# A fused attention and triangle kernel: a new loop for the closing stage, and a new order of the last instructions before each triangle stage

## Chip, cores, metric

One Trainium2 chip, one core. The metric is device time in microseconds (us) of one execution. Every number is from runs in the fast state; the mean granted clock of a run was 0.99 to 1.00 in all profiles, though it is lower in some short stretches (one matters below). Engines: PE (matrix), DVE (vector), ACT (scalar), POOL (GpSimd), SP (issues DMAs).

## The reference

Float32 throughout, x is (4, 64, 64, 256): four batches of 4096 tokens. Layer 0 is self-attention over 4096 tokens; layer 1 is a triangle attention over a 64 x 64 grid with eight heads, followed by two layer norms around a small MLP.

```python
# layer 0, per batch
f, g, v = xt @ Wf + bf, xt @ Wg + bg, xt @ Wh + bh
o = softmax(g @ f.T) @ v @ Wo + bo
x = x + o
# layer 1, per batch
q, k, v1, v2 = (x @ W for W in (Wq, Wk, Wv1, Wv2))      # heads of 32
att = softmax(einsum('bilhd,bljhd->biljh', q, k) / sqrt(32), axis=2)
out = einsum('biljh,bilhd,bljhd->bijhd', att, v1, v2)
h = layer_norm(x + out @ Wo)
return layer_norm(relu(h @ W1 + b1) @ W2 + b2 + h)
```

## The kernel before

It goes through the batches one by one: layer 0 (PE bound), then a triangle stage of 32 steps (products on DVE and POOL, PE accumulates). What follows the triangle (output projection, norm, MLP, norm) is done in 16 pieces of 256 tokens, one batch late, in the gaps of the next batch's triangle. Only the last batch has nothing after it to hide in, so its pieces 48 to 63 run in a closing stage, `alone`.

The end of layer 0, where the projections of the last 512 tokens are staged in tiles of tag "R" (three buffers):

```python
stage = [work.tile([P, 4, QB], F32, tag="R", name="stage", bufs=3) for _ in range(3)]
... # cut
score(3)
proj(last, "q", 1, None, stage[1][:, 3, :], nc.scalar)
proj(last, "k", 1, None, stage[2][:, 0, :], nc.scalar)   # stored from the ACT queue
L.fetch_qk(1)
hidden(1)                      # 8 matmuls, 2 relus of an old piece
L.sums(0); L.weights(0)        # softmax sums (DVE), eight scalings (ACT)
proj(last, "v2", 1, None, stage[2][:, 1, :], nc.scalar)
L.turn(0); L.stationary(0)     # transposes (PE), copies attP and wsel (ACT)
```

A product of a triangle step writes a tile of the same tag:

```python
R = work.tile([P, D, N], F32, tag="R", name="R", bufs=3)
nc.vector.tensor_tensor(R, src.unsqueeze(1).to_broadcast([P, D, N]), v2[:, h], ALU.mult)
```

The closing stage, and the tiles that matter in it:

```python
# h: one buffer (tag "h"); z: two (tag "s4"); far loads of A and y: tag "R"
def residue(tt):   # POOL, two instructions
    z = h * lag + (lab + b2)
def finish(tt):    # POOL, two instructions, then a store from SP
    z = z * log + lob
def alone(t0, t1):
    for n in range(2): heads(t0 + 1, n)
    for tt in range(t0 + 2, t0 + 5): load(tt, True)
    stats_a(t0 + 1); roots(0, 2); polish(0, 2, V)
    for tt in range(t0, t1):
        if before: hidden(tt, ...); rectify(tt, ...)            # PE, 4 relus on ACT
        if one:    affine_a(tt + 1)                             # h, ACT
        if before: affine_o(tt - 1); finish(tt - 1)             # z, ACT
        if two:    heads(tt + 2, ...); load(tt + 5, True)       # PE
        if one:    turn(tt + 1); residue(tt + 1)
        outputs(tt, 0); outputs(tt, 1)                          # PE
        if two:    stats_a(tt + 2)
        stats_o(tt)
        roots(k0, 4); polish(k0, 4, V)      # both norms in one go
    ... # cut: the last piece, in two halves
```

In the names of the profile: `heads` is the output projection of a piece (tile hp), `turn` a transpose (htp), `hidden` and `outputs` the two products of the MLP (mp, zp), `rectify` its relus (hid), and `roots` with `polish` makes the factor of a norm (rn).

## Time and profile before

| what | value |
|---|---|
| time, three runs before the prediction | 3957.36, 3961.72, 3963.80 us |
| span of the profiled run | 3958.3 us |
| PE's last accumulation of the triangle to the first outputs of the closing stage | 3768.9 to 3783.6 us |
| first outputs to the end | 3783.6 to 3958.3 us, 174.7 us |

The views that carry the argument (the chain of waits, the timeline, the windows) are in the prediction. A line of the chain has a start, a duration and what held the end at that time. A line of the timeline has a start, a duration, engine, source line and tiles; in brackets how long the engine had idled and who released it. In a window's line, after the span, each engine's busy time is followed by its count.

### The profile page before, as it was taken

Reading aid. Unit: us, or ns where it says so; the run is one execution under the profiler, and the core shown is the slowest. Engines: PE = TensorE matmul, PEld = TensorE weight load, DVE = VectorE, ACT = ScalarE, POOL = GpSimd, SP = SyncE. Lnnn points to the kernel's source line nnn. Section 1 sums busy time; section 2 is a strip of 40 time slices with the busy share of each in tenths; the row PEclk is TensorE's granted clock in tenths of the full one; section 3 lists DMA queues with packets and bytes.
Section 4 is the critical chain, followed back from the end, with each engine's and each line's share of the span. In section 5 each row is a group of like instructions: output and inputs, shape, how many; then the busy total and the mean of one; then the engine's idle time right before and its main releaser. Section 6 shows DMA issues by size and latency. Waiting matters only on the chain.

```text
span 3958.3 us, 59208 instructions
## 1 busy us (share of the span) xinstructions
PE 3742.3 (95%) x23302; PEld 1746.5 (44%) x23302; DVE 2692.7 (68%) x2193; ACT 1812.4 (46%) x3747; POOL 1927.2 (49%) x1024
## 2 busy tenths in 40 slices
PE   9999998889999999998999999999899999999987
PEld 5444444433444444443344444444344444444376
DVE  4444399896445399998444459999644448999944
ACT  3333455554333455554433345555433335555444
POOL 4000098893000199998000049999400008999944
PEclk9999999999999999999999999999999999999999
DMA  4111445552111523323111154233211143331121
GB/s 118 49 51 51 120 131 137 134 146 95 46 53 48 129 66 90 84 52 104 34 51 51 51 135 93 52 84 76 69 51 51 48 110 84 87 85 47 39 74 49
DMA packets 439711, 309.36 MB, mean 78 GB/s; under 512 B 299328, under 2 KB 404544, under 8 KB 432128
## 3 DMA queue, kind: packets, MB, share of 16 engines
q1 hardware_dynamic: 419952, 291.12, 27.8%
q10 hardware_dynamic: 16240, 8.59, 0.8%
q0 software_dynamic: 3232, 5.78, 0.6%
q8 instruction: 186, 3.05, 0.3%
q14 instruction: 101, 0.83, 0.1%
HBM read 165.88 MB, written 139.46 MB: 77 GB/s over the span
## 4 chain that ended last, share of the span: by engine, by line
PE 73%; ACT 8%; DVE 7%; DMA 4%; POOL 3%; issue 3%; SPq 2%; ACTq 0%; POOLq 0%; DVEq 0%
PE o L432 23%; PE acc L808 12%; PE proj L489 8%; PE s L410 7%; PE mp L954 5%; PE zp L969 4%; DVE R L799 4%; PE v1p L514 3%; PE sp L704 3%; POOL Rp L799 3%; ACT S L714 2%; PE hp L861 2%; ACT ao L816 2%; SPq L823 1%; PE y L474 1%
## 5 line engine op out<-in xcount | busy, mean ns | idle before, releaser
L799 POOL TENSOR_TENSOR Rp<-attP,v 128x2048 f32<-128x2048 f32 x328 | 1490.3, 4572 | 459.3 <-ACT attP L758 375.7
L799 DVE TENSOR_TENSOR R<-att,v 128x2048 f32<-128x2048 f32 x696 | 1547.3, 2273 | 102.2 <-ACT attP L758 45.3
L439 DVE TENSOR_TENSOR esum<-esum,e 128x2048 f32<-128x2048 f32 x224 | 512.8, 2289 | 583.4 <-ACT e L421 580.4
L808 PE MATMUL acc<-R,wsel 128*32 128x512 f32 x5568 | 728.3, 605 | 70.5 <-DVE R L799 46.9
L421 ACT ACTIVATE e<-s 128x1024 f32<-128x1024 f32 x512 | 496.6, 1021 | 403.5 <-PE s L410 381.7
L900 POOL TENSOR_SCALAR nt<-mv 128x4 f32<-128x4 f32 (+1 forms) x51 | 9.8, 193 | 1283.6 <-DVE mv L878 1279.5
L816 ACT COPY ao<-acc 128x1024 f32<-128x1024 f32 x256 | 261.4, 1021 | 548.5 <-PE acc L808 462.4
L432 PE MATMUL o<-e,vlo 128*128 128x512 f32 x1024 | 473.7, 605 | 0.0
L432 PE MATMUL o<-e,vhi 128*128 128x512 f32 x1024 | 472.6, 605 | 0.0
L808 PE MATMUL acc<-Rp,wsel 128*32 128x512 f32 x2624 | 346.8, 603 | 34.6 <-POOL Rp L799 34.4
L808 PEld LDWEIGHTS acc<-R,wsel 128*32 128x32 f32 x5568 | 142.6, 109 | 400.2 <-issue 205.0
L432 PEld LDWEIGHTS o<-e,vlo 128*128 128x128 f32 x1024 | 184.0, 189 | 280.8 <-issue 280.8
L432 PEld LDWEIGHTS o<-e,vhi 128*128 128x128 f32 x1024 | 184.3, 189 | 279.7 <-issue 279.7
L410 PE MATMUL s<-gT,fT 32*128 32x512 f32 x2048 | 302.2, 640 | 4.9 <-ACT e L421 4.5
L954 PE MATMUL mp<-hT,w 128*128 128x256 f32 x1024 | 250.5, 390 | 39.3 <-ACT hT L934 39.3
L741 ACT ACTIVATE es<-S,rd 128x64 f32<-128x64 f32 x1024 | 258.4, 338 | 29.3 <-DVE rd L733 28.6
L451 DVE RECIPROCAL rec<-den 128x512 f32<-128x512 f32 x32 | 107.4, 3358 | 215.6 <-PE den L449 215.6
L969 PE MATMUL zp<-w,hid 128*128 128x256 f32 x1024 | 246.2, 386 | 0.6 <-ACT hid L961 0.6
L954 PEld LDWEIGHTS mp<-hT,w 128*128 128x128 f32 x1024 | 182.9, 189 | 117.1 <-ACT hT L934 57.5
L969 PEld LDWEIGHTS zp<-w,hid 128*128 128x128 f32 x1024 | 187.1, 191 | 62.3 <-issue 40.2
L501 ACT COPY st<-proj 128x512 f32<-128x512 f32 x104 | 61.0, 586 | 293.1 <-issue 165.9
L410 PEld LDWEIGHTS s<-gT,fT 32*128 32x128 f32 x2048 | 83.0, 182 | 193.7 <-issue 173.3
(153 smaller groups left out, 3783.9 us busy)
## 6 DMA issues: line engine op xcount, KB each, us to landing
v<-v2d SPq DMA_DIRECT2D x24, 1024.0 KB, 12.3
v1c<-v1d SPq DMA_DIRECT2D x128, 128.0 KB, 2.9
aT<-ao SPq DMA_DIRECT2D x1024, 16.0 KB, 1.9
A<-aT SPq DMA_DIRECT2D x256, 64.0 KB, 2.0
out_dram<-z SPq DMA_DIRECT2D x63, 256.0 KB, 2.2
y<-yT SPq DMA_DIRECT2D x56, 256.0 KB, 2.1
q<-st SPq DMA_DIRECT2D x56, 256.0 KB, 2.6
v1d<-st SPq DMA_DIRECT2D x56, 256.0 KB, 2.1
```

The source lines that it names most:

```text
L410: nc.tensor.matmul(s_ps[r // 2][:, r % 2, :], fT[rows, tt, ts(n, P)], gT[rows, ts(qb, QB)], start=True, stop=not safe,)
L421: nc.scalar.activation(e[g][:, 2 * j : 2 * j + 2, :], s_ps[j], AF.Exp)
L432: nc.tensor.matmul(o_ps[qb], F.v[tt][:, r * 4 + n, :], es[:, r, :], start=(k == 0 and r == 0), stop=(k == 7 and r == 3),)
L439: nc.vector.tensor_tensor(esum[qb], esum[qb], es, ALU.add)
L489: nc.tensor.matmul(ps, w[:, cc, rows], y(qb, cc), start=(cc == 0), stop=(cc == 1))
L514: nc.tensor.matmul(ps[:, ts(n, C)], y(qb, cc)[:, ts(m * 2 + n, P)], wv1_sb[:, cc, :], start=(cc == 0), stop=(cc == 1),)
L741: nc.scalar.mul(self.e[:, i, :], rows[:, i, :], rec[:, i : i + 1])
L799: eng.tensor_tensor(R, src.unsqueeze(1).to_broadcast([P, D, N]), v2[:, h], ALU.mult)
L808: nc.tensor.matmul(acc[32 * c : 32 * c + 32, n % 2, :], w[:, n, c, 16 * h : 16 * h + 32], R[:, ts(c, 8), :].rearrange("p d j -> p (d j)"), ...
L816: nc.scalar.copy(self.ao[step][:, ts(np, 2)].rearrange("p k d j -> p k (d j)"), acc)
L954: nc.tensor.matmul(self.mp[:, fc % 2, :], w1_sb[:, cc, ts(fc, P)], self.hT[tt][:, cc, :], start=(cc == 0), stop=(cc == 1),)
L969: nc.tensor.matmul(self.zp[tt][:, n, :], self.hid[tt][:, fc, ts(n, P)], w2_sb[:, fc, :], start=(fc == 0), stop=(fc == 3),)
```

## The change

Intent: in the closing stage, make the first norm of a piece a whole piece ahead, apart from the second norm of an older piece; load ahead into big tiles that the last heads no longer use; begin on the last piece's first half as soon as it is there. And at the opening of a triangle stage, make the first weights before other work.

```diff
         proj(last, "q", 1, None, stage[1][:, 3, :], nc.scalar)
+        L.sums(0)
         proj(last, "k", 1, None, stage[2][:, 0, :], nc.scalar)
         L.fetch_qk(1)
+        L.weights(0)
         hidden(1)
-        L.sums(0)
-        L.weights(0)
-        proj(last, "v2", 1, None, stage[2][:, 1, :], nc.scalar)
         L.turn(0)
         L.stationary(0)
+        proj(last, "v2", 1, None, stage[2][:, 1, :], nc.scalar)
@@ load(tt, far=True)
-                both = work.tile([P, 2, 2, 256], F32, tag="R", name="A", bufs=3)
+                tag = ("v2", "S", "qk")[t % 3]
+                both = big.tile([P, 2, 2, 256], F32, tag=tag, name="A", bufs=1 if tag == "qk" else 2)
@@ alone (old loop cut)
+            self.stats_a(t0 + 1)
+            normed(0, 2)
+            self.affine_a(t0 + 1)
+            for tt in range(t0, t1 - 1):
+                if tt + 2 < t1:
+                    for n in range(2):
+                        self.heads(tt + 2, n, psum=pc)
+                    self.stats_a(tt + 2)
+                    if tt + 5 < t1:
+                        self.load(tt + 5, True)
+                self.turn(tt + 1)
+                self.residue(tt + 1)
+                if tt + 2 < t1:
+                    normed(0, 2)
+                    self.affine_a(tt + 2)
+                for n in range(2):
+                    self.outputs(tt, n)
+                mps = [self.hidden(tt + 1, fc, wide=True) for fc in range(4)]
+                self.stats_o(tt)
+                normed(2, 4)
+                for fc in range(4):
+                    self.rectify(tt + 1, fc, mps[fc])
+                self.affine_o(tt)
+                self.finish(tt)
... (cut: the last piece's halves go to two PSUM banks; heads of piece 49 are made just before alone)
@@ run_layer1
+            if b == NB - 1 and step in (28, 29, 30):
+                rest.load(t1 + step - 27, True)
```

More of the change, by code (lines that the diff above doesn't have):

```diff
@@ L963, in rectify, with outputs @@
             )
-        def outputs(self, tt, n):
+        def outputs(self, tt, n, apart=None):
             if n == 0:
                 self.zp[tt] = pb("zp").rearrange("p (n c) -> p n c", n=2)
+            zp = self.zp[tt]
+            if apart is not None:
+                zp = self.zp[tt + 1] = apart("zp").rearrange("p (n c) -> p n c", n=2)
             for fc in range(4):
                 nc.tensor.matmul(
-                    self.zp[tt][:, n, :], self.hid[tt][:, fc, ts(n, P)], w2_sb[:, fc, :],
+                    zp[:, n, :], self.hid[tt][:, fc, ts(n, P)], w2_sb[:, fc, :],
                     start=(fc == 0), stop=(fc == 3),
@@ L985, in alone, with normed @@
             V = nc.vector
-            for n in range(2):
-                self.heads(t0 + 1, n, psum=pc)
-            for tt in range(t0 + 2, t0 + 5):
-                self.load(tt, True)
+            def normed(k0, k1):
+                self.roots(k0, k1)
+                self.polish(k0, k1, V)
             self.stats_a(t0 + 1)
-            self.roots(0, 2)
-            self.polish(0, 2, V)
-            for tt in range(t0, t1):
-                one, two, before = tt + 1 < t1, tt + 2 < t1, tt > t0
-                if before:
-                    mps = [self.hidden(tt, fc, wide=True) for fc in range(4)]
-                    for fc in range(4):
-                        self.rectify(tt, fc, mps[fc])
-                if one:
-                    self.affine_a(tt + 1)
-                if before:
-                    self.affine_o(tt - 1)
-                    self.finish(tt - 1)
-                if two:
+            normed(0, 2)
@@ L1005, in alone @@
+            self.affine_a(t0 + 1)
+            for tt in range(t0, t1 - 1):
+                if tt + 2 < t1:
                     for n in range(2):
                         self.heads(tt + 2, n, psum=pc)
-                    self.load(tt + 5, True)
-                if one:
-                    self.turn(tt + 1)
-                    self.residue(tt + 1)
-                if not one:
-                    break
+                    self.stats_a(tt + 2)
[6 more added lines that the diff above has]
+                    self.affine_a(tt + 2)
@@ L1013, in alone @@
                 for n in range(2):
                     self.outputs(tt, n)
-                if two:
-                    self.stats_a(tt + 2)
+                mps = [self.hidden(tt + 1, fc, wide=True) for fc in range(4)]
                 self.stats_o(tt)
-                k0 = 0 if two else 2
-                self.roots(k0, 4)
-                self.polish(k0, 4, V)
+                normed(2, 4)
+                for fc in range(4):
+                    self.rectify(tt + 1, fc, mps[fc])
+                self.affine_o(tt)
@@ L1022, in alone @@
+                self.finish(tt)
+            tt = t1 - 1
             z = self.z[tt]
+            self.outputs(tt, 0)
+            self.outputs(tt, 1, pc)
             for n in range(2):
-                self.outputs(tt, n)
-            for n in range(2):
-                V.tensor_tensor(z[:, n], self.zp[tt][:, n], z[:, n], ALU.add)
+                V.tensor_tensor(z[:, n], self.zp[tt + n][:, n], z[:, n], ALU.add)
                 self.stats(z, 2, (n,))
-                self.roots(2 + n, 3 + n)
-                self.polish(2 + n, 3 + n, V)
+                normed(2 + n, 3 + n)
@@ L1183, in run @@
                     rest.ios.append(L.io)
+            for n in range(2):
+                rest.heads(NP * (NB - 1) + 1, n, psum=pc)
             rest.alone(NP * (NB - 1), NP * NB)
```

## The prediction

> **What bounds the kernel now.** I read the page first. TensorE (PE) is busy in nearly every slice, and only the last slices sag:
>
> ```profile
> PE 3742.3 (95%) x23302; PEld 1746.5 (44%) x23302; DVE 2692.7 (68%) x2193; ACT 1812.4 (46%) x3747; POOL 1927.2 (49%) x1024
> PE   9999998889999999998999999999899999999987
> ```
>
> A change of two short stages can therefore move the total only by what those stages lose. Next I read the chain of work that ended last, from 3768 us on, which is the closing stage ("alone": the last batch's 16 pieces of 256 tokens, without the triangle products). It opens with a hole: PE ends at 3771.3, the first far load is issued only behind the eight stores of the last step, and PE gets its data 6.5 us later.
>
> ```profile
> 3775.14 0.52 SPq L851
> 3775.71 1.97 DMA A<-aT
> 3777.82 2.23 PE hp L861 x4
> ```
>
> Then come 14 nearly equal rounds. One of them, in the same view (start, us, what):
>
> ```profile
> 3846.62 3.47 PE zp L969 x16
> 3850.17 0.70 DVE z L885
> 3850.90 0.44 DVE st L877
> ...
> 3852.68 1.05 DVE nt L901
> ...
> 3853.95 1.14 DVE nt L903
> ...
> 3855.77 1.03 ACT h L913 x2
> 3856.84 0.55 PE htp L931 x3
> 3857.39 3.47 PE zp L969 x16
> ```
>
> The reader is to see that a round is a closed loop. Both norms share one small Newton step (the "polish", nt and rn), so the h of the next piece waits for the z of this one: second product, sum, statistics, polish, h, transpose, second product. From outputs of piece 50 (3804.29) to those of piece 62 (3931.23) it takes 126.9 us, or 10.58 a round. PE itself needs less: zp 3.47, mp 3.47, hp 2 x 1.08 (two starts in the timeline, 3832.17 and 3833.25), htp 0.55, in sum 9.65. So 0.93 us a round is lost. The windows of two rounds agree:
>
> ```profile
> 3825.42:3846.62 21.20, 19.89 (x97) 16.78 (x97) 11.88 (x32) 9.95 (x25) 10.14 (x8) 1.00 0.27 75
> ```
>
> PE has 19.89 of 21.20 at full granted clock; ACT and POOL are half busy. A second ring lies close behind, on POOL, in the timeline:
>
> ```profile
> 3847.08 1.27 POOL L977 TENSOR_TENSOR z<-z,log_bc 128x512 f32<-128x512 f32 x1 [3.00 <-ACT z L913]
> 3848.43 1.27 POOL L978 TENSOR_TENSOR z<-z,lob_bc 128x512 f32<-128x512 f32 x1
> 3852.43 1.26 POOL L943 TENSOR_TENSOR z<-h,lag_bc 128x512 f32<-128x512 f32 x1 [2.74 <-DMA out_dram<-z]
> ```
>
> z has two buffers, so POOL can begin the residual of piece t+2 only when piece t has been stored. Before the change this wait costs nothing, since h of the following piece comes still later: L943 ended at 3832.40 and h began at 3834.47.
>
> The third view is the chain at the start of a triangle stage (batch 1; batches 2 and 3 read the same), and the list of DMA issues:
>
> ```profile
> 1375.09 0.84 ACT hid L961 x2
> ...
> 1377.82 0.48 ACT stage L501
> ...
> 1378.32 9.06 DMA v2d<-stage
> ...
> 1387.41 2.29 DVE R L799
> ```
> ```profile
> v2d<-stage ACTq DMA_DIRECT2D x8, 256.0 KB, 9.1
> k<-stage ACTq DMA_DIRECT2D x4, 256.0 KB, 10.7
> ```
>
> The third product of VectorE (DVE) writes a buffer (tag R, three of them) that held the last k and v2 projections. It waits until their stores have landed, not for the weights.
>
> **What the Trainium skill says.** "SBUF — State Buffer", section "Who interferes with whom": a DVE instruction with two SBUF inputs, or in a 2-port mode, and a GpSimd instruction that reads SBUF exclude each other for a whole instruction. The trace agrees: L901 takes 0.16 us alone and 1.05 here, ending at 3853.73 as POOL's L943 ended at 3853.69; L903 ends as L944 does. That is about 1.9 us inside the old loop. "DMA: Bandwidth & Descriptors", section "Anatomy of one DMA — SWDGE (gpsimd) path": some 2.0 us fixed plus bytes over 436e3, which for 256 KB gives an estimate of 2.6; from the end of L978 to the start of L943 I count 2.29 to 2.74 in this trace, once 4.26, with a mean of 2.50 over 15. (These stores come from SP, so another issuing path, about the same time.) The same page, "Queues, rings and completion order": an engine takes turns between the queues and goes in order within one. The trace fits: k, issued on the ACT queue at 1373.97 with a median of 10.7, lands near 1384.7, and v2 behind it lands at 1387.4, which is 2.7 later, near the 2.5 us of an undisturbed v2 store.
>
> **The change part by part.**
>
> (1) The opening hole. Loads of pieces 50, 51 and 52 now go out in steps 28 to 30, into tiles of the v2, S and qk tags that no longer have readers; those stores of aT are long done. Heads of piece 50 can follow those of 49 at 3771.3. I then went down the new order of each engine with durations of the trace: h(49) ready at 3775.4 (as before), outputs(48) at 3776.05 (before 3783.73), hidden(49) to 3782.97, outputs(49) at 3785.68 (before 3793.76). POOL finishes z(48) at 3788.4, the store lands at 3790.8, residual(50) L943 ends at 3792.05, and h(51) may begin at 3792.1. Outputs(50) come 2.95 us later, at 3795.05, against 3804.29: **-9.2 us**. (Why 2.95 is under 2.)
>
> (2) The round. The first norm now has its own polish, a piece ahead, and leaves the loop: the two blocked DVE instructions no longer delay h. If nothing else bound, a round would be PE's 9.65. But the second ring remains, and got longer. h has one buffer, so h(t+3) waits until POOL's L943 has read h(t+2), which waits for the store of z(t); and in the new order of ACT there stand between h and the affine of z the Ln and Exp of the second norm and the four relus. The built program has exactly these waits: the residual on a DMA semaphore, h on one of POOL. The sum from the end of one affine of z to the end of the next: 0.08 to POOL; L977 to L978 1.35; L978 1.26; store 2.50; L943 1.27; to ACT 0.05; two h issue in 0.92; Ln 0.33; Exp 0.11 (the next ACT instruction started that soon after a small one at 1356.3); four relus issue in 1.45; two affines end after 1.08. That is **10.40 us**, above 9.65, so this is the new bound: 12 rounds give 124.8 against 126.9, **-2.1 us**. Outputs start when the relus end, 0.92 + 0.33 + 0.11 + 1.57 + 0.02 = 2.95 after h began. The polish of the second norm is ready 2.67 after h began, before ACT needs it at 2.81; barely beside the path.
>
> (3) The last piece. Outputs go to two PSUM banks, so DVE can start on the first half after 8 of 16 matmuls, 1.73 sooner; but POOL's finish of piece 62 then runs at the same time, and I charge 0.4 for blocked DVE instructions: **-1.3 us**.
>
> (4) First weights of a triangle stage, four times. ACT makes the eight es (2.0 us) right after the copy of k, before two relus (0.84) and not after them, and the transposes come before v2's projection. The first product starts some 1.5 us sooner (0.7 in batch 0, where there are no relus). But the chain above does not go through it: v2's copy now stands behind attP (0.32) and four copies of wsel (1.0), so its store is issued at about 1379.1 instead of 1378.3. As it queues behind k's until 1384.7 anyway, it lands where it did. In batch 0 the second product waits for q's store, issued as before, to 495.4. So **0 us**, plus or minus 0.8 each.
>
> Sum: -9.2 - 2.1 - 1.3 + 0 = -12.6; 3961.7 - 12.6 = **3949 us**, 0.3% less.
>
> **The rivals.** (a) The ring through z's buffers isn't the bound, and rounds run at PE's 9.65: 12 x 0.93 = 11.2 in place of 2.1, total 3940. For it speaks PE's high share and that a change meant for this should reach it; against it the ring's sum, in which no term is guessed by more than 0.1. (b) The ring is longer than I make it, 10.8 (late polish blocked by POOL, slow stores, which now count in full where old slack hid them): +2.6 in place of -2.1, total 3954. The single store of 4.26 speaks for it. (c) Part 4 isn't neutral: if the later issue carries through, 4 x 0.8 = +3, total 3952; if the third product's wait was set by something that also moves up, 4 x 1.5 = -6, total 3943. The nine to eleven microseconds of those stores while the DMA engines are full speak against both. (d) Early loads in steps 28 to 30 hold up stores on the same queue: five issues of about 0.6 are 3 us in a step of 15; a slip of 1 to 2 us at most.
>
> **Range and chances.** (a) and (b) span 3940 to 3954; adding part 4 and 2 us of scatter between runs (three runs lie 6.4 apart) I take 3941 to 3957. All of it is within 0.6% of before. Over 2% would be 79 us, about half of the whole closing stage of 187 us; neither part can give or cost that.
>
> **What would show it.** Right: in the profile after, no hole at the opening of the closing stage, outputs(48) some 7 us after the last accumulation of the triangle (15 before); then rounds of about 10.4 whose chain goes POOL L982, L983, store, POOL L945, ACT h, relus, z, with POOL's L945 waiting on the store and the outputs of PE waiting on the relus about 0.7 a round. Wrong: rounds of 9.65 with PE unbroken (rival a), or the chain through the polish of the second norm (rival b). For part 4: the first product of batch 1 about 1.5 us sooner against the stage's opening, the third at an unchanged distance, and its wait still on v2's store. The prediction is wrong if rounds leave 10.1 to 10.7, or if the triangle stages shift by over 1 us each.

## The result, and the profile after

3939.66 us median (3938.07 to 3942.44, 4 runs) against 3960.93 (4 runs), ratio 0.9947 with a 95% interval of 0.9930 to 0.9965: 21 us faster where 12.6 were forecast, and below the stated range. A ratio is the mean time of one kernel's fast runs over that of the other's of the same rounds, so it is not quite the ratio of the medians.

The two traces, by milestones (us; the third column is what that part gained):

| part | before | after | gain | forecast |
|---|---|---|---|---|
| start to the last accumulation of the triangle | 3768.92 | 3762.06 | 6.9 | 0 |
| from there to outputs of piece 50 | 35.2 | 25.9 | 9.3 | 9.2 |
| outputs 50 to outputs 62 | 126.9 | 121.6 | 5.3 | 2.1 |
| outputs 62 to the end | 27.3 | 26.7 | 0.6 | 1.3 |

The opening of the closing stage after, in the chain of waits. It answers to the hole that the prediction shows: heads of piece 50 follow those of 49 with no load between.

```profile
3760.21 1.85 PE acc L808 x16
3762.07 1.06 PE hp L863 x4
...
3763.34 0.87 PE hp L863 x4
...
3767.51 1.03 ACT h L915 x2
...
3769.13 3.46 PE zp L974 x16
```

The hole cost more than its idle time. Before, the first four matmuls of the heads behind it took 2.23 us (in the prediction's lines); in the timelines such four took 1.03 to 1.13 ahead of it, and as long after the change. The windows show the granted clock (third number from the end) at about half. Before, then after:

```profile
3776.00:3784.00 8.00, 6.16 (x18) 4.41 (x19) 0.99 (x4) 0.23 (x1) 2.06 (x2) 0.53 0.71 176
```
```profile
3762.00:3770.00 8.00, 6.34 (x37) 5.20 (x34) 3.44 (x16) 3.36 (x7) 1.27 (x1) 1.00 0.21 57
```

A round after, in the timeline, first ACT, then POOL:

```profile
3837.18 1.55 ACT L963 ACTIVATE hid<-mp,b_sb 128x256 f32<-128x256 f32 x4
3838.61 1.10 ACT L915 ACTIVATE z<-z,rn 128x256 f32<-128x256 f32 x2
...
3846.07 1.02 ACT L915 ACTIVATE h<-hp,rn 128x256 f32<-128x256 f32 x2 [5.03 <-DVE nt L902]
```
```profile
3839.78 1.27 POOL L982 TENSOR_TENSOR z<-z,log_bc 128x512 f32<-128x512 f32 x1 [2.63 <-ACT z L915]
3841.13 1.26 POOL L983 TENSOR_TENSOR z<-z,lob_bc 128x512 f32<-128x512 f32 x1
3844.77 1.27 POOL L945 TENSOR_TENSOR z<-h,lag_bc 128x512 f32<-128x512 f32 x1 [2.37 <-DMA out_dram<-z]
```

The reader is to see the forecast ring: z, finish, store, residual (L945), h (L915), and from there relus and z again. L945 ends at 3846.04 and h starts at 3846.07. The bracket on h names DVE's L902, and so does the list of waits in ten rounds of eleven. L902 is an instruction that POOL's L945 had blocked, so both end within some 0.03 us, and the trace can't say which of them released h; an experiment below can.

The opening of the triangle stage of batch 1, DVE's products in the timeline, before and then after:

```profile
1379.08 2.29 DVE L799 TENSOR_TENSOR R<-att,v 128x2048 f32<-128x2048 f32 x1 [6.45 <-ACT attP L758]
...
1382.12 2.28 DVE L799 TENSOR_TENSOR R<-att,v 128x2048 f32<-128x2048 f32 x1
1387.41 2.29 DVE L799 TENSOR_TENSOR R<-att,v 128x2048 f32<-128x2048 f32 x1 [3.01 <-DMA v2d<-stage]
```
```profile
1373.72 2.29 DVE L799 TENSOR_TENSOR R<-att,v 128x2048 f32<-128x2048 f32 x1 [4.70 <-ACT attP L758]
...
1376.76 4.48 DVE L799 TENSOR_TENSOR R<-att,v 128x2048 f32<-128x2048 f32 x2
...
1383.91 4.49 DVE L799 TENSOR_TENSOR R<-att,v 128x2048 f32<-128x2048 f32 x2 [1.59 <-DMA v2d<-stage]
```

Before, the third product waits for the store of v2. After, the third runs right behind the second ("x2"), and the fourth waits. Measured from the stage's first sums (1371.71 before, 1368.09 after), the store has landed by 15.7 and 15.8, so in this batch the landing is where the prediction put it. What stands in front of it is not: a product (2.2 us) and the statistics behind it (1.1 us) now fill the wait. As a mark I use the third softmax sums of a stage on DVE ("the sums of step 2", steps counted from 0), which come behind all products of the first step. They come 27.35 us after the first sums before and 24.21 after, so 3.1 us sooner. In batches 0 to 3 it is 1.3, 3.1, 3.1 and 0.0: in batch 3 of this profile the store landed 3.2 later than before, and in batch 0 the second product still waits for q's store.

Why the third product no longer waits can be read in the addresses of the built programs. Before, the three stages lie at 139648, 156032 and 147840, and products 1, 2, 3 get these addresses in this order, so the third gets that of k and v2. In the changed program the stages lie at 156032, 139648 and 147840, products 1 and 2 get the first two, the third gets 156032 again (the first product's), and only the fourth 147840. The pool's choice followed the new order of the program; no line of the diff asks for it.

### The profile page after: what moved, and what is told of

Same layout as the page of the kernel before. It is cut to its first block, busy times and chain, and to the rows that moved or that the text cites. A ratio compares the mean times of both kernels' runs of the same rounds, so it can differ in the third digit from the quotient of the medians.

```text
span 3936.3 us, 59354 instructions
## 1 busy us (share of the span) xinstructions
PE 3737.0 (95%) x23302; PEld 1742.6 (44%) x23302; DVE 2708.9 (69%) x2291; ACT 1814.4 (46%) x3775; POOL 1927.0 (49%) x1024
## 4 chain that ended last, share of the span: by engine, by line
PE 72%; ACT 9%; DVE 6%; DMA 5%; POOL 3%; issue 3%; SPq 3%; ACTq 0%; POOLq 0%; DVEq 0%
PE o L432 24%; PE acc L808 12%; PE proj L489 8%; PE s L410 7%; PE mp L956 5%; PE zp L974 3%; DVE R L799 3%; PE sp L704 3%; PE v1p L514 3%; POOL Rp L799 2%; ACT S L714 2%; ACT ao L816 2%; SPq L823 2%; PE hp L863 2%; PE y L474 1%
## 5 line engine op out<-in xcount | busy, mean ns | idle before, releaser
L902 POOL TENSOR_SCALAR nt<-mv 128x4 f32<-128x4 f32 (+1 forms) x51 | 9.9, 193 | 1283.6 <-DVE mv L880 1279.5
```

## The experiments

Twelve runs, eleven edited kernels and the changed kernel once more, each timed in five rounds against the kernel before, in three calls on three chips. All gave correct results. Theory A, rival B and rival C are named in the expectations.

| run | median, us | before, us | ratio (95%) |
|---|---|---|---|
| closing_only | 3944.16 | 3960.48 | 0.9958 (0.9945 to 0.9972) |
| front_only | 3952.12 | 3960.48 | 0.9981 (0.9973 to 0.9989) |
| weights_early_v2_first | 3958.61 | 3960.48 | 0.9993 (0.9985 to 1.0002) |
| v2_late_weights_late | 3957.28 | 3960.48 | 0.9997 (0.9989 to 1.0005) |
| loads_early_only | 3955.58 | 3962.13 | 0.9984 (0.9978 to 0.9991) |
| z3 | 3943.19 | 3962.13 | 0.9954 (0.9941 to 0.9967) |
| h2 | 3927.86 | 3962.13 | 0.9914 (0.9902 to 0.9927) |
| stores_apart | 3927.08 | 3962.13 | 0.9911 (0.9897 to 0.9926) |
| after_again | 3934.38 | 3960.19 | 0.9945 (0.9931 to 0.9958) |
| before_apart | 3951.09 | 3960.19 | 0.9980 (0.9973 to 0.9987) |
| z3_h2 | 3934.23 | 3960.19 | 0.9950 (0.9937 to 0.9964) |
| best | 3915.14 | 3960.19 | 0.9892 (0.9877 to 0.9907) |

Single executions of these kernels scatter by some 5 us to either side (before: 3954.7 to 3966.2 in 35 runs; loads_early_only more, 3942.7 to 3966.8). Where the scatter comes from is not shown: the landing times described below vary, and in those 35 runs the slower ones also show a lower mean clock (0.990 to 0.993, correlation -0.7), of which either could be the effect of the other. So small effects are read in the traces too, by distances inside a stage.

### Which part gained: closing_only, front_only

Edits: the diff's parts, one at a time.

> The closing stage of the change alone, opening of the triangle stages as before. Theory A (the change's gain of 21 us is about 15 in the closing stage and 6 to 7 at the openings of the triangle stages, by the moved wait of the third product): 15 us faster than before, between 12.5 and 17.5, with the third product of batches 1 to 3 waiting for v2's store as before. Rival B (the gain seen before the closing stage in one profile was luck of transfers): 20 to 22 us faster.

> The opening of the triangle stages of the change alone. Theory A: 6 us faster than before, between 3 and 9; the third product waits no longer for a store and the fourth does. Rival B: within 1.5 us of before.

Measured: 0.42% and 0.19%, which is 16.6 us (11 to 22) and 7.5 us (4 to 11) of 3960. Their sum, 24, agrees with the 21 of both within the intervals. The gain ahead of the closing stage belongs to the change and is no luck of one profile: rival B falls for the front. (Its size in one profile is partly luck: steps 2 to 31 of batch 0 took 389.9 to 393.1 us in the ten traces whose h and z keep their buffers, and no edit there touches these steps.) In the trace of closing_only the third product of batches 1 to 3 waits for v2's store as before, and the time from first outputs to the end is 167.6 us, as in the changed kernel (167.3) and unlike before (174.7).

### Sooner weights, or the moved wait: weights_early_v2_first, v2_late_weights_late, before_apart

```diff
 # weights_early_v2_first, against before
+L.sums(0)
 proj(last, "k", 1, ...)
 L.fetch_qk(1)
+L.weights(0)
 hidden(1)
-L.sums(0)
-L.weights(0)
 proj(last, "v2", 1, ...)
```
```diff
 # v2_late_weights_late, against before
-proj(last, "v2", 1, ...)
 L.turn(0)
 L.stationary(0)
+proj(last, "v2", 1, ...)
```

> Sums and weights made sooner as in the change, but v2's last projection stays ahead of the transposes. In the built program the third product then keeps the buffer of the last k and v2 and so the wait for v2's store. Theory A (the wait that moved pays, not the sooner weights): 0 to 1 us faster, although the first product starts some 1 us sooner. Rival C (the sooner weights pay, 1.5 us for each stage): 4 to 6 us faster.

> Only v2's last projection moved behind the transposes; sums and weights as late as before. In the built program the third product then takes the buffer of the first and the fourth takes that of k and v2. Theory A: 3 to 7 us faster, nearly all of what the opening alone gives, although v2's store is issued over 1 us later. Rival C: 0, or up to 3 us slower for the later store.

Sooner weights alone: 0.07%, from 6 us faster to 1 us slower, so the clock by itself excludes neither forecast. The trace decides: in batch 1 the first product starts 6.65 us after the first sums and not 7.37, the third waits for the store until 15.73, and the sums of step 2 come at 27.37 (before 27.35). So a sooner first product by itself buys nothing here, and rival C falls.

The later v2 alone: 0.03%, with an interval of 4 us faster to 2 us slower. This miss counts against my size of 3 to 7 us, though not against the mechanism: in the trace the third product runs right behind the second in every batch, and the sums of step 2 come at 25.55, 24.46 and 25.84. v2's store is issued 10.0 to 10.6 us after the first sums (before 6.6, in the changed kernel 7.4), since its copy queues behind late weights on ACT, and the fourth product starts at 17.17, 15.90 and 17.45. I took this for the reason of the miss, that the two moves need one another, but it is not shown: these starts are no later than front_only's and the changed kernel's (15.43 to 18.86), and the gains of the two single moves, with their intervals, do not exclude the gain of both. The profiled execution was the second fastest of 13, so its total isn't used. The size of this move alone stays open: about 1 us a stage at most by the clock, 1.3 to 2.9 in the trace.

The direct test takes the wait away in the old order:

```diff
 # before_apart, against before: staged in tag "st", not in tag "R"
-proj(last, "q", 1, None, stage[1][:, 3, :], nc.scalar)
-proj(last, "k", 1, None, stage[2][:, 0, :], nc.scalar)
-proj(last, "v2", 1, None, stage[2][:, 1, :], nc.scalar)
+proj(last, "q", 1, None, None, nc.scalar)
+proj(last, "k", 1, None, None, nc.scalar)
+proj(last, "v2", 1, None, None, nc.scalar)
```

> Before, in its old order everywhere, with the last q, k and v2 projections staged in tiles of another tag. If the wait of the third product for v2's store was worth what the change gained at the openings: the sums of step 2 come 3 us sooner in each of batches 1 to 3 and 4 sooner in batch 0, 10 to 15 us faster than before in sum. If the transfers' load only moves the wait: within 3 us of before.

Measured: 0.20%, 8 us (5 to 11), below the 10 to 15 expected, with an interval that reaches into it. The sums of step 2 come at 24.76, 24.21 and 24.98 in batches 1 to 3 (2.3 to 3.1 sooner) and at 19.95 and not 23.72 in batch 0, where the second product's wait for q's store goes too, which the change keeps. In batches 1 to 3 that is 8.0 us in this trace, where the change gained 6.3 in its own. So taking away the wait for the store, with no weights made sooner, is worth what the change gains at these openings.

Chance gave one more case. In the profiled run of loads_early_only (next paragraph; its openings are the old ones, with the old addresses), v2's store of batch 3 landed unusually early, before the third product was due:

```profile
3276.59 4.48 DVE L799 TENSOR_TENSOR R<-att,v 128x2048 f32<-128x2048 f32 x2
```

There the sums of step 2 came at 24.84 and not at 27.25. In the traces of all runs this store landed between 12.2 and 18.8 us after the first sums, in batches 1 to 3. (With the staging in tag R, batch 3 shows 17.0 to 18.8 in the six traces of the changed order and 12.2 to 17.2 in the four that keep v2 in its old place.)

### The opening hole: loads_early_only

Edit: only the `load` hunk and the `run_layer1` loads of the diff, with the old loop.

> Before, with only the far loads of the closing stage moved into tiles of v2, S and qk, the first three in steps 28 to 30; the loop of the closing stage is the old one. By the prediction's part 1: 6.5 to 8 us faster, the hole at the opening gone, rounds still 10.55. If the hole had been hidden by something later in the old loop: under 2 us.

Measured: 0.16%, 6.3 us (4 to 9). In the trace outputs of piece 50 come 7.7 us sooner behind the last accumulation. Rounds are 10.5 to 10.6, one 10.25 (outputs 50 at 3793.98, outputs 62 at 3920.07, so 126.1). Part 1 of the prediction stands, for the loads alone. Its rival (d), loads that hold up stores, did not come: from the sums of step 28 of the last batch to the last accumulation it is 75.3 us here and 75.3 in closing_only and front_only; before and after both have 76.4.

### What bounds the new round: h2, z3, z3_h2

```diff
 # h2, against the changed kernel (and the same for the other user of the tag)
-self.h[tt] = work.tile([P, 2, C], F32, tag="h", name="h", bufs=1)
+self.h[tt] = work.tile([P, 2, C], F32, tag="h", name="h", bufs=2)
```
```diff
 # z3, against the changed kernel (and the same for the other user of the tag)
-z = self.z[tt] = work.tile([P, 2, C], F32, tag="s4", name="z")
+z = self.z[tt] = work.tile([P, 2, C], F32, tag="s4", name="z", bufs=3)
```
```diff
 # z3_h2: z3, and (two more buffers don't fit) a second, idle tag for h
+tag = "yc" if tt > NP * (NB - 1) + 1 and tt % 2 else "h"
```

> The changed kernel with two buffers for h in place of one; z keeps two. If the ring needs both links (the store frees z, and h waits for the residual that waits for the store), cutting it at h gives the same: rounds of about 9.51 and 27 to 29 us faster than before. If only the store matters to later instructions some other way, or the blocked DVE instructions set the round: as the changed kernel, 20 to 22 faster than before.

> The changed kernel with three buffers for z (and its tag) in place of two. If the ring through z's buffers (store of the last piece but one, residual, h, relus, affine) bounds the changed loop: rounds fall from 10.17 to PE's 9.51, 11 rounds of 0.66, so 6 to 8 us faster than the changed kernel, 27 to 29 faster than before. If instead DVE instructions blocked by POOL set the changed round, as the chain of waits names nt: under 1.5 us better than the changed kernel.

> The changed kernel with three buffers for z, and two for h by a second tag in the closing stage. If with three z buffers the round is set by DVE's polish of the first norm, blocked by four POOL operations that then run one behind another: rounds stay near 10.33 and the time near that of three z buffers alone, 17 to 21 us faster than before. If it was the wait of h for its single buffer there too: rounds of 9.51 and 28 to 32 us faster than before.

h2 makes rounds of 9.51, PE unbroken, and takes 157.1 us from first outputs to the end where the changed kernel takes 167.3. These 10.2 us are most of its gain over it (13 by the ratios of two calls); 34 us (29 to 39) faster than before, more than the 27 to 29 expected, since the last two rounds fell as well (7.64 and 7.86 for 10.15 and 9.35). So h's single buffer is a link of the ring, and it was POOL's L945 that released h, not DVE's L902. In h2, h starts ahead of L945:

```profile
3842.22 1.02 ACT L915 ACTIVATE h<-hp,rn 128x256 f32<-128x256 f32 x2 [2.27 <-DVE rn L910]
```
```profile
3843.66 1.27 POOL L945 TENSOR_TENSOR z<-h,lag_bc 128x512 f32<-128x512 f32 x1 [2.35 <-DMA out_dram<-z]
```

One window each, of one round of h2 and of z3:

```profile
3838.09:3847.60 9.51, 9.51 (x51) 8.38 (x49) 8.65 (x24) 5.39 (x15) 5.06 (x4) 1.00 0.30 84
```
```profile
3831.11:3841.44 10.33, 9.78 (x49) 8.39 (x49) 8.02 (x23) 5.26 (x15) 5.03 (x4) 1.00 0.29 78
```

z3 was a miss: I expected the same gain from a third buffer for z. L945 waits for no store there, and yet a round takes 10.33, longer than the changed kernel's 10.17; 18 us (13 to 23) faster than before, no better than the changed kernel. The timeline of z3 shows what took the store's place (POOL, DVE and ACT in order of time):

```profile
3834.69 1.15 DVE L904 TENSOR_TENSOR nt<-nt 128x2 f32<-128x2 f32 x1
3835.78 1.27 POOL L945 TENSOR_TENSOR z<-h,lag_bc 128x512 f32<-128x512 f32 x1
...
3835.87 1.20 DVE L905 TENSOR_SCALAR nt<-nt 128x2 f32<-128x2 f32 x1
...
3837.12 1.27 POOL L946 TENSOR_TENSOR z<-z,lb_bc 128x512 f32<-128x512 f32 x1
3837.30 1.12 DVE L909 TENSOR_TENSOR rn<-mv,rn 128x2 f32<-128x2 f32 x1
...
3838.71 1.02 ACT L915 ACTIVATE h<-hp,rn 128x256 f32<-128x256 f32 x2 [4.25 <-DVE rn L910]
```

POOL's four instructions now run one behind another. The polish of the first norm falls into them, and three of its instructions take 1.1 to 1.2 us where they take 0.16 to 0.20 undisturbed; each ends as a POOL instruction ends. In the changed kernel the store's 2.3 us had parted the four, and most of the polish ran in the gap. z3_h2 tells this apart from a wait for h's buffer: with two buffers for h as well, a round still takes 10.32 (3824.58 to 3834.90) and h starts behind DVE's rn. Its time, 20 us (14 to 25) faster by the ratio and 26 by the medians, lies with the changed kernel's and not with h2's; by the medians it is above the 17 to 21 expected, and the round, the sharper measure, decides. The two buffers of z with their store thus do a service here: they space POOL's work. A wait that one removes can be replaced by a longer one on another path, and only the trace of the edited kernel shows it.

### Both repairs: stores_apart, best, after_again

stores_apart is the edit of before_apart on the changed kernel, best is that with h2.

> The changed kernel with the last q, k and v2 projections staged in tiles of another tag, so that no product of a first step waits for their stores. Theory A: the second product of batch 0 starts some 3 to 6 us sooner, the fourth of batches 1 to 3 by 1.5 to 4.5: 6 to 14 us faster than the changed kernel, 27 to 35 faster than before. If the DMA engines' load at that time only moves the wait to another transfer: within 2 us of the changed kernel.

> The changed kernel unaltered, once more, for a larger sample and a second trace: 19 to 23 us faster than before. In the trace, batches 1 to 3 start the third product right behind the second, and the fourth when v2's store has landed, 15.4 to 19 us after the stage's first sums; rounds of the closing stage 10.17.

> The changed kernel with two buffers for h and with the last q, k and v2 staged in another tag. If both gains add: 41 to 49 us faster than before, about 3917 us; if the closing stage's gain is eaten by a shifted wait: about 3927, as with the staging alone.

stores_apart: 35 us (29 to 41) faster than before, at the top of the 27 to 35 expected. No product of a first step waits for a store. From the timeline of best, batch 1 (first sums at 1370.4), where the four DVE products behind the first run in two groups with only the statistics between:

```profile
1379.09 4.45 DVE L799 TENSOR_TENSOR R<-att,v 128x2048 f32<-128x2048 f32 x2
...
1384.55 4.45 DVE L799 TENSOR_TENSOR R<-att,v 128x2048 f32<-128x2048 f32 x2
```

The sums of step 2 come at 22.5 us in batches 1 to 3 of both kernels, 1.7 sooner than in the changed kernel where the store was early, and 4.7 sooner in its profiled batch 3, where the store landed at 18.9. Only now does the sooner first product pay too: 22.5 against 24.2 to 25.0 in before_apart.

after_again: 0.55%, 22 us (17 to 27), so the result repeats; 3934.38 in this call against 3939.66 in the first shows how far two calls differ. Its fourth products start at 15.79, 15.22 and 17.32, within the expected limits but for the second, and rounds are 10.17.

best: 3915.14 us, 1.08% or 43 us (37 to 49) faster than before, and the fastest kernel of this study. Both gains add, within the intervals.

## Why the prediction was wrong, step by step

- **Part 1, the opening hole: right, at the last step by luck.** -9.2 forecast to outputs of piece 50, -9.3 in the profile; loads alone give 6.3 by the clock and 7.7 in the trace, the rest is in the first two rounds (9.51 each for 10.05 and 10.53). I had outputs of piece 50 come 2.95 after h(51), when the relus end; they came 3.07 after it (3784.92, 3787.99), but because PE was busy until then. The granted clock of 0.53 behind the old hole was in the trace, and the forecast does not name it.
- **Part 2, the round: the mechanism right, the size off.** The ring was forecast and h2 shows its link at h. Its length was 10.17, not 10.40: I put in the mean store of 2.50 with its outliers (I count 14 stores, not 15), and the changed rounds show 2.29 to 2.37, with one 3.03. PE's own round was 9.51, not 9.65, and outputs begin after the first of the four relus (0.5 us after the relus start: 3837.18 and 3837.69), not after all, so the ring closes later than I had it: of the twelve rounds the first two took 9.51 and 9.68, nine 10.15 to 10.23 and one 10.88. In sum -5.3, not -2.1. Rival (a), rounds at PE's pace, is what h2 makes and the change doesn't, except in the first three rounds (outputs 48 to 51, 9.51 each), before the ring closes.
- **Part 3, the last piece:** -0.6 and not -1.3; small, not tried by itself.
- **Part 4, the openings of the triangle stages: wrong, and the step that fails the total.** I wrote that the third product "writes a buffer ... that held the last k and v2 projections" and that the store "lands where it did. ... So 0 us". The landing was right in batches 1 and 2; in batch 3 the store landed 3.2 later. (The time of k's landing behind it is from batch 0, the only one that the trace shows.) That the third product would go on waiting for it was taken over from the old program without looking; the built new program, which I had, gives it another buffer and moves the wait to the fourth. Worth 7.5 us by front_only, 6.9 in the profile. Of the 9.5 us by which the two traces differ from the forecast, this step is 6.9 and the round 3.2; part 3 takes 0.7 back. Of the rivals, (c) had the sign and roughly the size (-6), but by luck: its reason was that what releases the third product would move up with the weights; what happened is that the wait passed to the fourth.
- The chance of a change under 2% (0.99) and the claim that neither stage can hold 79 us were right.

Left open: how much v2's move is worth with late weights, where that run's clock and trace disagree, what the scatter of single executions is made of, and why the store's landing varies by over 6 us between batches and runs.

## What to carry to other kernels

When instructions are moved past each other in a program whose tiles come from a pool, compare the buffers that the built program hands out before and after, not only the order: a wait for a buffer can move to another instruction without a line that says so. When a wait at a stage's start is for a store's landing, put the staged data where the first consumers don't write; in this kernel the sooner work before it showed a gain only then. And before giving a buffer to break a ring, ask which link spaces the work of engines that exclude each other: here the same ring opened with a second h and not with a third z.

## What the Trainium skill lacked or had wrong

- "SBUF — State Buffer", "Who interferes with whom", agrees with the rounds shown: polish instructions of 2 elements per partition take 0.16 us alone and 0.9 to 1.2 under a POOL instruction of 1.27. What it lacks is a remark for the reader of a trace, and I found it on no other page: the blocked DVE instruction ends with its blocker (L902 by its start and duration at 3835.83, L945 at 3835.81), so a release that belongs to POOL is put down to DVE. The changed kernel's list of waits did so:

```profile
ACT h L915 <- DVE nt L902: 49.8, 10, 5.0
```

- "DMA: Bandwidth & Descriptors", "Anatomy of one DMA — SWDGE (gpsimd) path", has a fit for the GpSimd path alone. For 256 KB stored from SP, with the DMA engines busy 0.3 of the time, the runs show mostly 2.29 to 2.37 us from the end of the last writer to the start of the waiting instruction, some 0.3 under the estimate of 2.6 that the fit gives.
- I found no page that tells how far the landing of a large store moves behind other transfers: the same 256 KB store of v2, with a DMA share of 0.9 or more between issue and landing, landed 8.3 to 11.4 us after its issue in three batches of one profile.
